# GNN sums with the features on the partitions: gathered rows as the stationary side, one addition per group of edges

## The chip, the cores and the metric

The kernel runs on one core of a Trainium2 chip. A core has five engines that run their own instruction streams and wait for each other by semaphores: PE (TensorE, matrix products; its weight loads are listed apart as PEld), DVE (VectorE), ACT (ScalarE), POOL (GpSimd) and SP (which here only issues transfers). A matrix product has a stationary side, which is loaded into PE, and a moving side, whose columns are streamed past it. The metric is the device time of one execution in microseconds (us).

## The reference

Two layers follow each other on 12500 nodes with 256 features each (`x`, f32). A sparse mixture of experts stands behind a graph convolution:

```
z   = layernorm(x)
agg = segment_sum(z[src] * edge_weight[:, None], dst, 12500)   # 200000 edges, dst sorted
x   = x + agg @ W.T + b
y   = layernorm(x)
# gate: graph attention over 131072 other edges gives each node scores for 4 experts,
# the two best of them get softmax weights
x   = x + sum over 4 experts of gate * (gelu(y @ W1 + b1) @ W2 + b2)   # 256 -> 512 -> 256
```

All of it is f32. The change concerns the second line and the product with `W` behind it. In the inputs the destinations are denser for small node numbers, so that a run of consecutive edges reaches few nodes.

## The kernel before

**Front** (0 to 141 us). The 200000 edges are cut into 1563 chunks of 128 and 261 groups of six chunks (`GQ`). `src`, `dst` and `edge_weight` are loaded and turned so that a chunk's edges lie on the 128 partitions. `x` is normalised in 25 groups of four tiles of 128 nodes (six buffers; loads on SP's queue, L93; statistics on DVE, L104) and written to the table `z_rows` in DRAM (L316). Woven into that loop stands `windows()` (L235), which works out on DVE, for each group of edges, the first node that it reaches, the tile of 128 nodes that this node lies in (`tile0`), each edge's place in a window of 128 places (`lo_q`: the node number modulo 128, raised by 128 where the edge lies 128 or more nodes beyond the first, so that it matches nothing), and two masks `in0` and `in1` that say which places of the window belong to that tile and which to the next one. It also counts groups that reach over more nodes than one window (`more`).

**Edge stage** (141 to 2223 us). For each group POOL issues six indirect gathers (`gt<-z_rows`, L550 in `prepare`), each of 128 rows of 256 f32; three groups' rows fit into the buffers. DVE builds the one-hot rows of the edges' places (`hit_w`, L340), ACT scales each by its edge's weight (`oh_w`, L556). In `product` (L564) PE adds up six products in one PSUM tile `win` of 128 places x 256 features, with the one-hot rows `oh_w` as the stationary side and the 256 features of the gathered rows moving. An f32 product runs as two instruction pairs of load and product. `add_window` (L571) then adds `win` to `acc_x`, the sums of all nodes (128 nodes of a tile on the partitions, 99 tiles, 256 features), twice per group: to tile a under the mask `in0`, and to tile a + 1 under `in1`. Between these steps the stage runs another work: a sort of the 131072 edges of the attention (`count_all`, then `sort_all`: L340, L428 to L498). The order on PE, DVE and ACT is written out by hand for this stage (`tc.manual_schedule`); POOL follows its own program order. Behind it stand a CAST of the sort's result (L608) and a branch (L614) for groups that reach beyond one window; no instruction of its body runs on these inputs.

**Node stage** (2231 to 2453 us). Its order is a scheduler's, from a loop over groups of four node tiles with lags:

```python
for g in range(NG + 3):
    for stage, lag in ((node_load, -2), (node_out, 1), (node_norm, 2), (node_turn_back, 3),
                       (node_turn, 0), (node_gat, 3)):
```

`node_load` loads `x` for two groups and adds the bias on POOL (L707). `node_turn` turns `acc_x` on PE (L686) and copies it out of PSUM on ACT (L687), into `agt`. `node_out` multiplies by the turned `W` (L725) and adds `x` on DVE (L727), then takes statistics (L104, L105). `node_norm` forms `y` on DVE (L739). `node_turn_back` turns `y` (L686, L687) and stores it. `node_gat` forms the attention's values (PE L753, DVE L756 to L762), stores them (L765), and issues four scatters per group on POOL (L767) into the table of segment starts.

**The rest** (2453 us to the end): a scan over the segment starts, the experts (PE is busy nearly throughout; POOL gathers the attention's rows, L809), and the weighted sum with its transfers.

Of the kernel before, what the change touches and what calls it, by code (L numbers as in the profile page):

```python
# [34 lines left out]
P = 128  # L35
# [25 lines left out]
def gnn_gat_moe(ctx, tc, x, src, dst, edge_weight, W, b, W_gat, att_src, att_dst, b_gat, ln_gamma,  # L61
# [98 lines left out]
    wide = tc.alloc_tile_pool(name="wide", bufs=1)  # L160
    acc_x = wide.tile([P, NT + 1, D], F32, name="acc_x")
    for k in range(0, NT + 1, 3):
        nc.gpsimd.memset(acc_x[:, k:k + 3, :], 0.0)
    with ExitStack() as s1:
# [61 lines left out]
        lo_q = edges.tile([P, NQ * GQ], BF, name="lo_q")  # L226
        tile0 = edges.tile([P, NQ + 1], I32, name="tile0")
        in0 = edges.tile([P, NQ], F32, name="in0")
        in1 = edges.tile([P, NQ], F32, name="in1")
        more = edges.tile([1, 5 * P], I32, name="more")  # L230
# [4 lines left out]
        def windows():  # L235


# [7 lines left out]
            nc.vector.tensor_copy(further_by, ahead)  # L245
            as_int = late.tile([P, NQ * GQ], I32, name="scratch")
            nc.vector.tensor_copy(as_int, dst_f)
            nc.vector.tensor_scalar(as_int, as_int, P - 1, None, ALU.bitwise_and)
            nc.vector.tensor_copy(lo_q, as_int)
            beyond = late.tile([P, NQ * GQ], F32, name="scratch")  # L250
            nc.vector.tensor_scalar(beyond, ahead.rearrange("p q j -> p (q j)"), float(P), float(P),
                                    ALU.is_ge, ALU.mult)
            nc.vector.tensor_add(lo_q, lo_q, beyond)
            nc.vector.tensor_copy(tile0[:, :NQ], first_f)
            within = late.tile([P, NQ], F32, name="within")
            as_int = late.tile([P, NQ * GQ], I32, name="scratch")
            nc.vector.tensor_scalar(as_int[:, :NQ], tile0[:, :NQ], P - 1, None, ALU.bitwise_and)
            nc.vector.tensor_copy(within, as_int[:, :NQ])
            nc.vector.tensor_scalar(tile0[:, :NQ], tile0[:, :NQ], 7, None, ALU.logical_shift_right)
            nc.vector.tensor_scalar(in0, within, part, None, ALU.is_le)  # L260
            nc.vector.tensor_scalar(in1, within, part, None, ALU.is_gt)

# [60 lines left out]
        for i in range(2):  # L323
            pt = bank()
            for o in range(2):
# [3 lines left out]
        nc.sync.dma_start(STARTS[:E2, :].rearrange("(p l) c -> p (l c)", p=P),  # L329
                          acc_x.rearrange("p t d -> p (t d)")[:, :L2 * SEG])  # L330

# [228 lines left out]
        def product(rows, hots, there):  # L560

            win = ps.tile([P, D], F32, name="win")
            for j, (r, h) in enumerate(zip(rows, hots)):
                i = nc.tensor.matmul(win, h, r, start=(j == 0), stop=(j == len(rows) - 1))  # L564
                if j == 0:
                    after_all(i, there)
            return win

        def add_window(at, win, m):
            to = acc_x[:, bass.ds(at, 1), :].rearrange("p o d -> p (o d)")  # L570
            return nc.vector.scalar_tensor_tensor(to, win, m, to, ALU.mult, ALU.add)  # L571

# [5 lines left out]
        with tc.manual_schedule(engines={mybir.EngineType.PE, mybir.EngineType.DVE,  # L578
                                         mybir.EngineType.Activation}):
            at, done, coming, win = (), 0, group(0), None  # L580
            for q in range(NQ + 1):
                was, win = win, product(*coming) if q < NQ else None
                if q:
                    a = at[(q - 1) % 4]
                    i0 = add_window(a, was, in0[:, q - 1:q])
                if q + 1 < NQ:
                    coming = group(q + 1)
                if q:
                    i1 = add_window(a + 1, was, in1[:, q - 1:q])
                    if q + 1 < NQ:  # L590
                        tc.declare_no_dep(i1.ins, i0.ins, reason="the next tile of nodes")
                if q < NQ and q % 4 == 0:
                    n = min(4, NQ - q)
                    _, at = nc.values_load_multi_w_load_instructions(
                        tile0[0:1, q:q + n], engines=(mybir.EngineType.DVE,), min_val=0,
                        max_val=NT - 1, skip_runtime_bounds_check_because=BOUND)
                for work, q0, q1, steps in parts:
                    if q == q0:
                        done = 0
                    while q0 <= q < q1 and done * (q1 - q0) < (q + 1 - q0) * steps:  # L600
                        next(work, None)
                        done += 1
            for work, *_ in parts:
                for _ in work:
                    pass
# [8 lines left out]
        with tc.If(further > 0):  # L614
            shift = edges.tile([P, 1], F32, name="shift")
            idx4 = edges.tile([P, GQ], I32, name="idx4")
            lo4 = edges.tile([P, GQ], F32, name="lo4")
            lob4 = edges.tile([P, GQ], BF, name="lob4")
            node4 = edges.tile([P, GQ], I32, name="node4")
            w4 = edges.tile([P, GQ], F32, name="w4")  # L620
            ahead4 = edges.tile([P, GQ], F32, name="ahead4")
            below4 = edges.tile([P, GQ], F32, name="below4")
            m01 = edges.tile([P, 2], F32, name="m01")
            with tc.For_i(0, NQ, 1) as q:
                nc.vector.memset(shift, 0.0)
                n = nc.values_load(more[0:1, bass.ds(q, 1)], min_val=0, max_val=NT,
                                   skip_runtime_bounds_check_because=BOUND)
                with tc.For_i(0, n, 1) as j:
                    nc.vector.tensor_scalar_add(shift, shift, float(P))
                    nc.vector.tensor_copy(idx4, src1[:, bass.ds(q * GQ, GQ)])  # L630
                    nc.vector.tensor_copy(w4, w1[:, bass.ds(q * GQ, GQ)])
                    nc.vector.tensor_copy(ahead4, further_by.rearrange("p q j -> p (q j)")[
                        :, bass.ds(q * GQ, GQ)])
                    nc.vector.tensor_copy(m01[:, 0:1], first_f[:, bass.ds(q, 1)])
                    nc.vector.tensor_scalar(lo4, ahead4, m01[:, 0:1], None, ALU.add)
                    nc.vector.tensor_copy(node4, lo4)
                    nc.vector.tensor_scalar(node4, node4, P - 1, None, ALU.bitwise_and)
                    nc.vector.tensor_copy(lo4, node4)
# [4 lines left out]
                    nc.vector.tensor_copy(m01[:, 0:1], in0[:, bass.ds(q, 1)])  # L643
                    nc.vector.tensor_copy(m01[:, 1:2], in1[:, bass.ds(q, 1)])
                    nc.vector.tensor_copy(lob4, lo4)
                    win = product(*prepare(idx4, lob4, w4, range(GQ)))
                    a = nc.values_load(tile0[0:1, bass.ds(q, 1)], engines=(mybir.EngineType.DVE,),
                                       min_val=0, max_val=NT - 1,
                                       skip_runtime_bounds_check_because=BOUND)
                    a = nc.s_assert_within(a + j + 1, 0, NT - 1, skip_runtime_bounds_check_because=BOUND)  # L650
                    add_window(a, win, m01[:, 0:1])
                    add_window(a + 1, win, m01[:, 1:2])

# [3 lines left out]
    with ExitStack() as s2:  # L657
# [51 lines left out]

        def node_turn(g):  # L710
            f, (t0, n, _) = flow[g], rows_of(g)
            f["agt"] = gp.tile([P, GT, 2, P], F32, name="agt", bufs=2)
            turn(lambda i: acc_x[:, t0 + i, :], n, f["agt"])

        def node_out(g):
# [5 lines left out]
            for i, m in pairs(n):  # L721
                po = ps.tile([P, 2, D], F32, name="po")
                for a in range(m):
                    for k in range(2):
                        nc.tensor.matmul(po[:, a, :], f["agt"][:, i + a, k, :], w_t[:, k, :],  # L725
                                         start=(k == 0), stop=(k == 1))
# [47 lines left out]
        node_load(1)  # L774
        for g in range(NG + 3):
            for stage, lag in ((node_load, -2), (node_out, 1), (node_norm, 2), (node_turn_back, 3),
                               (node_turn, 0), (node_gat, 3)):
                if 0 <= g - lag < NG and (lag >= 0 or g - lag >= 2):
# [425 lines left out]
```

## Time and profile before

| | |
|---|---|
| runs, us | 4192.93, 4193.42, 4193.94 (median 4193.42) |
| profiled execution, us | 4198.22 |
| its span, us | 4196.4 |
| its mean granted PE clock | 0.935 |
| busy over the span | PE 3552.0 us (85%), PEld 2610.1 (62%), DVE 2393.0 (57%), ACT 1421.4 (34%), POOL 2906.0 (69%) |

The lines that follow are from a page of one profiled execution and from queries of its trace. The page shows the span in 40 equal slices, with a digit for the busy tenths of each engine. A group line names the source line, the engine, the operation, output<-inputs and the count, then busy time and the mean duration of one in ns, then the idle time of the engine ahead of these instructions with what released it ("issue": nothing that the profile shows). A wait line gives the total, the number of waits and the longest, in us. A timeline line gives the start, the duration, engine, line, operation and shapes, and how many like instructions it joins ("x12"), with the idle time before it in brackets. All inner durations belong to this one execution.

### The profile page before, as it was taken

The numbers are of one execution on the slowest core, as the hardware profiler recorded it, in microseconds if no ns is written. First come the engines' busy times: TensorE is split into PE (matmuls) and PEld (weight loads), VectorE is DVE, ScalarE is ACT, GpSimd is POOL, SyncE is SP. The second block draws the span as 40 slices with busy tenths as digits, with TensorE's granted clock in tenths as the row PEclk, the third lists the DMA queues.
The fourth block names the chain that finished last, engine by engine and source line by source line (L and its number), as shares of the span: only waits on it lengthen the run. The fifth ranks groups of instructions, "written<-read, shape, count | busy, mean of one in ns | idle before, by whom it ended". The sixth has DMA issues, their size and how long they took to land. (4 is left out here: it accounts for less than half of the span.)

```text
span 4196.4 us, 54596 instructions
## 1 busy us (share of the span) xinstructions
PE 3552.0 (85%) x18969; PEld 2610.1 (62%) x18970; DVE 2393.0 (57%) x5474; ACT 1421.4 (34%) x3289; POOL 2906.0 (69%) x2855
## 2 busy tenths in 40 slices
PE   1466899999999999999998959999989999899545
PEld 0365676767766667767677836666656666566424
DVE  7566777878787878787778950221211202212477
ACT  4322445445545444545452211221212212212122
POOL 2577777777777777777776777777777777773440
PEclk6688999999999999999999969999999999999767
DMA  7433333333333333333335652222222222221698
GB/s 234 135 93 93 102 102 100 100 100 101 100 101 100 99 101 101 100 101 100 99 102 157 191 145 60 67 72 55 64 50 75 75 55 64 65 60 62 206 226 346
DMA packets 265845, 457.42 MB, mean 109 GB/s; under 512 B 67943, under 2 KB 168705, under 8 KB 264289
## 3 DMA queue, kind: packets, MB, share of 16 engines
q0 software_dynamic: 114128, 219.11, 21.4%
q1 hardware_dynamic: 111663, 207.52, 14.0%
q10 hardware_dynamic: 39778, 27.28, 2.1%
q8 instruction: 153, 2.51, 0.2%
q14 instruction: 123, 1.01, 0.1%
HBM read 334.05 MB, written 119.66 MB: 108 GB/s over the span
## 5 line engine op out<-in xcount | busy, mean ns | idle before, releaser
L550 POOL DMA_INDIRECT gt<-z_rows,src x1563 | 1605.2, 1027 | 592.2 <-issue 410.2
L809 POOL DMA_INDIRECT G<-gat_nodes,order x1024 | 1026.5, 1002 | 339.3 <-issue 289.0
L564 PE MATMUL win<-gt,oh_w 128*128 128x256 f32 x3126 | 770.1, 398 | 200.4 <-DMA gt<-z_rows,src 149.3
L564 PEld LDWEIGHTS win<-gt,oh_w 128*128 128x128 f32 x3126 | 598.0, 198 | 317.0 <-issue 188.4
L966 PE MATMUL po<-w,hh 128*128 128x256 f32 x3136 | 724.3, 385 | 51.4 <-ACT hh L948 38.3
L966 PEld LDWEIGHTS po<-w,hh 128*128 128x128 f32 x3136 | 605.5, 193 | 220.8 <-issue 87.1
L970 DVE TENSOR_TENSOR fo<-po,b 128x512 f32<-128x512 f32 x196 | 135.3, 690 | 1016.6 <-PE po L966 1016.6
L942 PE MATMUL ph<-yt,w 128*128 128x512 f32 (+1 forms) x1600 | 707.8, 586 | 2.8 <-DMA w<-in_L_ffn_W 2.8
L556 ACT ACTIVATE oh_w<-hit_w,w 128x128 f32<-128x128 bf16 x1563 | 500.9, 390 | 448.2 <-PE win L564 226.6
L490 DVE TENSOR_SCALAR st<-along,place_l,code 128x1024 bf16<-128x1024 f16 x1024 | 550.3, 578 | 162.3 <-PE perm L498 161.7
L948 ACT ACTIVATE hh<-ph,b 128x512 f32<-128x512 f32 (+1 forms) x400 | 249.3, 676 | 1001.6 <-PE ph L942 1001.5
L498 PE MATMUL perm<-st,to_p 128*128 128x512 bf16 x2048 | 524.1, 378 | 0.0
L942 PEld LDWEIGHTS ph<-yt,w 128*128 128x128 f32 x1600 | 305.0, 191 | 292.5 <-issue 277.9
L454 PE MATMUL look<-next,oht 98*128 98x128 f32 x2044 | 393.8, 300 | 0.0
L454 PEld LDWEIGHTS look<-next,oht 98*128 98x128 f32 x2044 | 309.6, 192 | 37.5
L462 ACT ACTIVATE next<-place 98x256 f32<-98x256 f32 x511 | 196.1, 384 | 345.1 <-PE place L459 344.3
L469 DVE TENSOR_TENSOR sel<-look,oh_lo 128x512 f32<-128x512 f32 x256 | 174.9, 683 | 186.4 <-PE look L454 185.2
L498 PEld LDWEIGHTS <-to_p 128*128 128x128 bf16 x2048 | 178.5, 97 | 122.3 <-DVE st L490 0.4
L571 DVE SCALAR_TENSOR_TENSOR acc_x<-win,in,acc_x 128x256 f32 x522 | 246.9, 473 | 8.7 <-PE win L564 8.6
L450 PE MATMUL look<-oh_lo,same_hi 128*128 128x128 bf16 x1024 | 228.1, 223 | 1.2 <-ACT next L462 1.0
L442 ACT ACTIVATE same_hi<-bank 128x512 bf16<-128x512 f32 x256 | 152.8, 597 | 215.2 <-PE bank L440 215.1
L340 DVE TENSOR_TENSOR oh_hi<-twice,hi 128x784 bf16<-128x784 bf16 x256 | 143.4, 560 | 100.6 <-PE place L364 100.5
(278 smaller groups left out, 3641.8 us busy)
## 6 DMA issues: line engine op xcount, KB each, us to landing
expert_rows<-fo SPq DMA_DIRECT2D x48, 1024.0 KB, 4.2
fo_in<-expert_rows SPq DMA_DIRECT2D x24, 2048.0 KB, 16.4
gt<-z_rows,src POOLq DMA_INDIRECT x1563
G<-gat_nodes,order POOLq DMA_INDIRECT x1024
xt<-in_x SPq DMA_DIRECT2D x24, 512.0 KB, 4.8
z_rows<-xt ACTq DMA_DIRECT2D x24, 512.0 KB, 4.6
x_two<-in_x SPq DMA_DIRECT2D x12, 1024.0 KB, 6.4
x_rows<-x_two SPq DMA_DIRECT2D x12, 1024.0 KB, 10.6
```

What stands on the lines that cost most here:

```text
L450: first = nc.tensor.matmul(look[:, i % GT + k, :], b["m"][:, i + k, :], one(b["ol"], i + k), start=True, stop=False)
L454: nc.tensor.matmul(look[:, i % GT + k, :], b["oht"][:, i + k, :], nxt[:, k, :], start=False, stop=True)
L490: last = nc.vector.tensor_scalar(st[:, k, :], along, b["l"][:, i + k:i + k + 1], code2[:, c:c + 1], ALU.is_equal, ALU.mult)
L498: first = nc.tensor.matmul(perm[:, h, :], one(b["p"], i + k), st[:, k, h * 512:(h + 1) * 512], start=(c == 0), stop=(c == NC2 - 1), skip_g ...
L550: there = [nc.gpsimd.indirect_dma_start(out=rows[j], out_offset=None, in_=Z, in_offset=IND(ap=idx[:, c:c + 1], axis=0)) for j, c in enumer ...
L556: there += [nc.scalar.activation(hots[j], one(hit, j), AF.Copy, scale=w[:, c:c + 1]) for j, c in enumerate(chunks)]
L564: i = nc.tensor.matmul(win, h, r, start=(j == 0), stop=(j == len(rows) - 1))
L571: return nc.vector.scalar_tensor_tensor(to, win, m, to, ALU.mult, ALU.add)
L809: i = nc.gpsimd.indirect_dma_start(out=G[:, t + 1, :], out_offset=None, in_=NODE, in_offset=IND(ap=order[:, t:t + 1], axis=0))
L942: i = nc.tensor.matmul(ph[:, :n], w_1[:, e, k, f * P:(f + 1) * P], yts[g][:, :n, k, :], start=(k == 0), stop=(k == 1))
L948: i = nc.scalar.activation(item["hh"][:, f, :n * P], ph[:, :n].rearrange("p t m -> p (t m)"), AF.Gelu, bias=b_1[:, e * NF + f:e * NF + f + 1])
L966: m = nc.tensor.matmul(po[:, a, :], item["hh"][:, f, i * P:(i + 1) * P], w_2[:, e, f, :], start=(f == 0), stop=(f == NF - 1))
```

## The change

`acc_x` is kept the other way round: 128 features on the partitions, two halves of features, and all nodes along the free dimension. In `product` the gathered rows are now the stationary side, one half of 128 features at a time, and the 128 scaled one-hot columns move. Each chunk so has two products of 128 columns where it had one of 256. A group's window starts exactly at its first node (`start`), at any place of the free dimension, so that `add_window` is one plain addition, without masks. `windows()` has less to work out: an edge's place is its distance from the first node. `node_turn` is gone, and the products of `node_out` read `acc_x` directly as their stationary side; the lags behind it are one smaller. The branch for far groups is shortened accordingly.

```diff
-    acc_x = wide.tile([P, NT + 1, D], F32, name="acc_x")
+    acc_x = wide.tile([P, 2, NPAD + P], F32, name="acc_x")
...
-            as_int = late.tile([P, NQ * GQ], I32, name="scratch")
-            nc.vector.tensor_copy(as_int, dst_f)
-            nc.vector.tensor_scalar(as_int, as_int, P - 1, None, ALU.bitwise_and)
-            nc.vector.tensor_copy(lo_q, as_int)
-            beyond = late.tile([P, NQ * GQ], F32, name="scratch")
-            nc.vector.tensor_scalar(beyond, ahead.rearrange("p q j -> p (q j)"), float(P), float(P),
-                                    ALU.is_ge, ALU.mult)
-            nc.vector.tensor_add(lo_q, lo_q, beyond)
-            nc.vector.tensor_copy(tile0[:, :NQ], first_f)
-            within = late.tile([P, NQ], F32, name="within")
-            as_int = late.tile([P, NQ * GQ], I32, name="scratch")
-            nc.vector.tensor_scalar(as_int[:, :NQ], tile0[:, :NQ], P - 1, None, ALU.bitwise_and)
-            nc.vector.tensor_copy(within, as_int[:, :NQ])
-            nc.vector.tensor_scalar(tile0[:, :NQ], tile0[:, :NQ], 7, None, ALU.logical_shift_right)
-            nc.vector.tensor_scalar(in0, within, part, None, ALU.is_le)
-            nc.vector.tensor_scalar(in1, within, part, None, ALU.is_gt)
+            nc.vector.tensor_copy(lo_q, ahead.rearrange("p q j -> p (q j)"))
+            nc.vector.tensor_copy(start[:, :NQ], first_f)
...
         def product(rows, hots, there):
-            win = ps.tile([P, D], F32, name="win")
+            win = ps.tile([P, 2, P], F32, name="win")
             for j, (r, h) in enumerate(zip(rows, hots)):
-                i = nc.tensor.matmul(win, h, r, start=(j == 0), stop=(j == len(rows) - 1))
-                if j == 0:
-                    after_all(i, there)
+                for k in range(2):
+                    i = nc.tensor.matmul(win[:, k, :], r[:, k * P:(k + 1) * P], h,
+                                         start=(j == k == 0), stop=(j == len(rows) - 1),
+                                         skip_group_check=True)
+                    if j == k == 0:
+                        after_all(i, there)
             return win
 
-        def add_window(at, win, m):
-            to = acc_x[:, bass.ds(at, 1), :].rearrange("p o d -> p (o d)")
-            return nc.vector.scalar_tensor_tensor(to, win, m, to, ALU.mult, ALU.add)
+        def add_window(at, win):
+            to = acc_x[:, :, bass.ds(at, P)]
+            return nc.vector.tensor_add(to, to, win)
...
                 if q:
-                    a = at[(q - 1) % 4]
-                    i0 = add_window(a, was, in0[:, q - 1:q])
+                    add_window(at[(q - 1) % 4], was)
                 if q + 1 < NQ:
                     coming = group(q + 1)
-                if q:
-                    i1 = add_window(a + 1, was, in1[:, q - 1:q])
-                    if q + 1 < NQ:
-                        tc.declare_no_dep(i1.ins, i0.ins, reason="the next tile of nodes")
...
-        def node_turn(g):
-            f, (t0, n, _) = flow[g], rows_of(g)
-            f["agt"] = gp.tile([P, GT, 2, P], F32, name="agt", bufs=2)
-            turn(lambda i: acc_x[:, t0 + i, :], n, f["agt"])
-
         def node_out(g):
...
-                        nc.tensor.matmul(po[:, a, :], f["agt"][:, i + a, k, :], w_t[:, k, :],
+                        nc.tensor.matmul(po[:, a, :],
+                                         acc_x[:, k, (t0 + i + a) * P:(t0 + i + a + 1) * P],
+                                         w_t[:, k, :],
                                          start=(k == 0), stop=(k == 1))
...
-        for g in range(NG + 3):
-            for stage, lag in ((node_load, -2), (node_out, 1), (node_norm, 2), (node_turn_back, 3),
-                               (node_turn, 0), (node_gat, 3)):
+        for g in range(NG + 2):
+            for stage, lag in ((node_load, -2), (node_out, 0), (node_norm, 1), (node_turn_back, 2),
+                               (node_gat, 2)):
```

The order that results in the changed kernel differs around the node stage. On DVE the CAST of the sort's result and the instruction behind it come after the branch, where the CAST stood ahead of it. On PE the products of three node groups (24 L725 products of f32) stand at the head of the stage. On POOL two bias additions (L707) with eight scatters (L767) behind them become one addition, one scatter, one addition, seven scatters.

More of the change, by code (lines that the diff above doesn't have):

```diff
@@ L160, in gnn_gat_moe @@
     wide = tc.alloc_tile_pool(name="wide", bufs=1)
-    acc_x = wide.tile([P, NT + 1, D], F32, name="acc_x")
+    acc_x = wide.tile([P, 2, NPAD + P], F32, name="acc_x")
+    acc_flat = acc_x.rearrange("p h n -> p (h n)")
     for k in range(0, NT + 1, 3):
-        nc.gpsimd.memset(acc_x[:, k:k + 3, :], 0.0)
+        nc.gpsimd.memset(acc_flat[:, k * D:(k + 3) * D], 0.0)
     with ExitStack() as s1:
@@ L226, in gnn_gat_moe @@
         lo_q = edges.tile([P, NQ * GQ], BF, name="lo_q")
-        tile0 = edges.tile([P, NQ + 1], I32, name="tile0")
-        in0 = edges.tile([P, NQ], F32, name="in0")
-        in1 = edges.tile([P, NQ], F32, name="in1")
+        start = edges.tile([P, NQ + 1], I32, name="start")
         more = edges.tile([1, 5 * P], I32, name="more")
@@ L329, in gnn_gat_moe @@
         nc.sync.dma_start(STARTS[:E2, :].rearrange("(p l) c -> p (l c)", p=P),
-                          acc_x.rearrange("p t d -> p (t d)")[:, :L2 * SEG])
+                          acc_flat[:, :L2 * SEG])
         s0.close()
@@ L594, in gnn_gat_moe @@
                     _, at = nc.values_load_multi_w_load_instructions(
-                        tile0[0:1, q:q + n], engines=(mybir.EngineType.DVE,), min_val=0,
-                        max_val=NT - 1, skip_runtime_bounds_check_because=BOUND)
+                        start[0:1, q:q + n], engines=(mybir.EngineType.DVE,), min_val=0,
+                        max_val=N - 1, skip_runtime_bounds_check_because=BOUND)
                 for work, q0, q1, steps in parts:
@@ L616, in gnn_gat_moe @@
             idx4 = edges.tile([P, GQ], I32, name="idx4")
-            lo4 = edges.tile([P, GQ], F32, name="lo4")
             lob4 = edges.tile([P, GQ], BF, name="lob4")
-            node4 = edges.tile([P, GQ], I32, name="node4")
             w4 = edges.tile([P, GQ], F32, name="w4")
@@ L622, in gnn_gat_moe @@
             below4 = edges.tile([P, GQ], F32, name="below4")
-            m01 = edges.tile([P, 2], F32, name="m01")
             with tc.For_i(0, NQ, 1) as q:
@@ L633, in gnn_gat_moe @@
                         :, bass.ds(q * GQ, GQ)])
[L634 to L638, printed above, removed]
                     nc.vector.tensor_scalar(ahead4, ahead4, shift, None, ALU.subtract)
@@ L642, in gnn_gat_moe @@
                     nc.vector.tensor_mul(w4, w4, below4)
-                    nc.vector.tensor_copy(m01[:, 0:1], in0[:, bass.ds(q, 1)])
-                    nc.vector.tensor_copy(m01[:, 1:2], in1[:, bass.ds(q, 1)])
-                    nc.vector.tensor_copy(lob4, lo4)
+                    nc.vector.tensor_copy(lob4, ahead4)
                     win = product(*prepare(idx4, lob4, w4, range(GQ)))
-                    a = nc.values_load(tile0[0:1, bass.ds(q, 1)], engines=(mybir.EngineType.DVE,),
-                                       min_val=0, max_val=NT - 1,
+                    a = nc.values_load(start[0:1, bass.ds(q, 1)], engines=(mybir.EngineType.DVE,),
+                                       min_val=0, max_val=N - 1,
                                        skip_runtime_bounds_check_because=BOUND)
-                    a = nc.s_assert_within(a + j + 1, 0, NT - 1, skip_runtime_bounds_check_because=BOUND)
-                    add_window(a, win, m01[:, 0:1])
-                    add_window(a + 1, win, m01[:, 1:2])
+                    a = nc.s_assert_within(a + j * P + P, 0, N - 1,
+                                           skip_runtime_bounds_check_because=BOUND)
+                    add_window(a, win)
     with ExitStack() as s2:
```

## The prediction

> **What bounds the kernel now.** I read the slices of the page first, then the groups and waits of the long middle stretch, then timelines of one group of edges and of one pair of node groups, and last the front.
>
> ```profile
> PE   1466899999999999999998959999989999899545
> POOL 2577777777777777777776777777777777773440
> ```
>
> A slice is 105 us. PE looks like the bound from slice 5 on, but POOL's 7 is also flat over slices 2 to 20, the edge stage (141 to 2223 us). The groups of POOL in the window 400 to 2200 us and the waits of POOL and PE there decide between them:
>
> ```profile
> L550 POOL DMA_INDIRECT gt<-z_rows,src x1364 | 1385.0, 1015 | 415.7 <-issue 357.8 <-DMA gt<-z_rows,src 19.8 <-PE place L459 13.1
> ```
> ```profile
> POOL gt L550 <- issue: 410.2, 1346, 0.3
> ```
> ```profile
> PE win L564 <- DMA gt<-z_rows,src: 111.9, 102, 2.3
> PE win L564 <- issue: 28.1, 34, 1.7
> ```
>
> Busy 1385.0 plus gaps 415.7 make 1800.7 us of a window of 1800, and no gap is longer than 0.3: POOL issues gather after gather, 1.320 us each, 7.92 us for a group of six. It never waits for a buffer, an index or PE. PE waits for the rows: 111.9 + 28.1 = 140 us over some 227 groups, 0.6 us each. So the edge stage is paced by the issue of 1563 gathers, which the change leaves alone; PE has a slack of 0.5 to 0.6 us a group, DVE more (busy 1421 of 1800). One group on PE and DVE, from the timeline:
>
> ```profile
> 2171.09 0.47 DVE L571 SCALAR_TENSOR_TENSOR acc_x<-win,in,acc_x 128x256 f32 x1
> ...
> 2173.64 2.46 PEld L564 LDWEIGHTS win<-gt,oh_w 128*128 128x128 f32 x12 [1.14 <-issue]
> ...
> 2173.67 2.83 PE L564 MATMUL win<-gt,oh_w 128*128 128x256 f32 x12 [0.99 <-DMA gt<-z_rows,src]
> ```
>
> Twelve load-and-product pairs of 256 columns take 2.83 us, 0.236 each. The node stage (2231 to 2453) is another matter: between 2253 and 2440 DVE is busy 182.3 of 187 us.
>
> **The change part by part.** *The products.* Six chunks with two halves, each f32 product still two pairs, give 24 pairs of a 128-wide load and 128 moving columns, where there were 12 with 256. Nearest rows, from timelines:
>
> ```profile
> 2170.42 0.22 PE L450 MATMUL look<-oh_lo,same_hi 128*128 128x128 bf16 x1
> 2170.48 0.44 PE L454 MATMUL look<-next,oht 98*128 98x128 f32 x2
> 2170.75 0.23 PE L450 MATMUL look<-oh_lo,same_hi 128*128 128x128 bf16 x1
> ```
> ```profile
> 2231.50 1.94 PE L686 MATMUL pt<-ident,acc_x 128*128 128x128 f32 x16 [1.47 <-DVEq L614]
> ...
> 2339.13 1.86 PE L753 MATMUL ph<-wg,yt 128*128 128x16 f32 x16
> ```
>
> L450 and two L454, three pairs of 128 columns, repeat after 0.33 us: 0.11 each. The sixteen turns of L686, each with a new f32 load and 128 columns, take 1.94, 0.121 each; L753, with 16 columns, is limited by loads, 0.116 each. So 24 pairs cost 2.78 to 2.90 us: −0.05 to +0.07 a group against 2.83, inside PE's 0.5. Worth nothing. Upper bound: if the load does not hide at all, a pair costs the whole 0.22 of L450's or half L454's row plus nothing else; that is 24 x 0.22 = 5.28, a rival below.
>
> *The additions.* 261 of 522 L571 go, 261 x 0.473 = 123 us of DVE, all beside POOL's gathers; what hides it is that gather stream, and uncovered it would be worth those 123 us. The remaining addition reads the same 128x256; its form (plain addition, two rows of 128 nodes) is new, and the nearest row, L727 with 0.69 for 512 columns, does not make it dearer than 0.47. A gather's busy time does depend a little on DVE (0.95 while DVE is idle, 1.015 in the mean), but the gathers beside L571 look like those without; I take 0, with ±10 for the whole stage from shifted coincidences. The last window's second addition and one CAST (below) do lie on the path.
>
> *The window table.* Removed from DVE: L247 0.976, L248 0.967, L249 0.966, L251 0.942, L253 1.778, L257 to L261 0.286 + 0.287 + 0.268 + 0.348 + 0.349 = 7.17 us; added: one CAST of 128x1566 f32 to bf16, 0.97 by L249's row. Net −6.2, in a stretch (40 to 70 us) where DVE has no idle time. Later DVE waits for x:
>
> ```profile
> DVE st L104 <- DMA xt<-in_x: 15.1, 10, 3.3
> ```
>
> Loads of x follow the release of six buffers, which follows the LN arithmetic, so some of the shift is passed on and some is lost in these waits. I take −4, bounds 0 and −6.2.
>
> *The boundary.* The order of the changed kernel puts the CAST of the permutation behind the branch, beside the node stage's first loads, and the last group has one addition.
>
> ```profile
> 2230.07 1.23 DVE L608 CAST st<-perm 128x1024 bf16<-128x1024 f32 x1 [0.22 <-PE perm L498]
> ...
> 2239.89 9.29 POOL L707 TENSOR_TENSOR x_two<-x_two,b_all 128x1024 f32<-128x1024 f32 x4 [17.22 <-DMA b_all<-in_L_gnn_b]
> ...
> 2242.27 0.69 DVE L727 TENSOR_TENSOR x_two<-x_two,po 128x512 f32<-128x512 f32 x1 [9.94 <-POOL x_two L707]
> ```
>
> The branch waits for it, and the issue of b_all's load follows; so up to 1.23 + 0.47 = 1.7 is gained, and I take 1.5, least 0. The first turns and copies are gone as well, but they were hidden: the first L727 waits for POOL's addition of b_all, not for PE.
>
> *The node stage.* Gone are the L686 turns of acc_x (196 instructions, 25.3 us of PE) and their 49 copies (26.7 us of ACT). Neither engine sets the pace. L725 reads acc_x directly, with the same loads. Two groups cost 16.96 us between like rows of DVE:
>
> ```profile
> 2329.77 0.69 DVE L727 TENSOR_TENSOR x_two<-x_two,po 128x512 f32<-128x512 f32 x1
> ...
> 2339.94 5.27 DVE L739 TENSOR_SCALAR y<-x_two,mv,rstd 128x256 f32<-128x256 f32 x1
> 2346.73 0.69 DVE L727 TENSOR_TENSOR x_two<-x_two,po 128x512 f32<-128x512 f32 x1
> ```
> ```profile
> 2340.40 4.65 POOL L707 TENSOR_TENSOR x_two<-x_two,b_all 128x1024 f32<-128x1024 f32 x2
> 2346.41 0.99 POOL L767 DMA_INDIRECT gat_starts<-nds,seg  x1 [1.36 <-DVE root L119]
> ```
>
> One normalisation, 0.38 elsewhere, takes 5.27: it stands until both of POOL's additions are over. So DVE's full time hides 4.9 us of standing still per two groups, while POOL in turn waits 1.36 + 1.28 for DVE before its scatters (8 x 1.27 = 10.2 us, and 4.65). With the lags one shorter, POOL's order becomes addition, one scatter, addition, seven scatters: DVE can work during the first scatter, and a second instruction can be caught. I take 0.6 us a pair of groups (half of that scatter's 1.27), 12 pairs: −7. Best case: POOL alone paces, 10.2 + 4.65 = 14.8, −2.1 x 12 = −25. Worst, both additions now catch DVE after it has had to wait for an addition: +0.7 x 12 = +8. The scatters' end releases the starts' load, the scans and the experts (PE again from 2494.9), with nothing else late, so the shift reaches the end. The run of experts and the mix are unchanged.
>
> Sum: −4 + 0 − 1.5 − 7 = −12.5, on the profiled execution's 4198.2 (span 4196.4): 4185.7. It lies 4.8 above the median of the runs, 4193.4, which goes to **4181**.
>
> **The rivals.** *Loads that do not hide (slower).* With the gathered rows stationary, every load is 128 columns for a product of only 128. PE's slack decides: (2.83 + 0.5) / 24 = 0.139 us a pair. At 0.16, 24 x 0.16 = 3.84, 0.5 beyond the slack, x 229 groups of the sorting part = +115; at 0.22, 1.95 x 229 = +445, about 4640. For: L564's product of 256 columns covers its next load twice over, one of 128 just once, with nothing to spare. Against: the rows above, all at or below 0.121. The Trainium skill, "TensorE: Matmul & The Clock Gate", Part 3 "Packing small matmuls — row/col tiling", The mechanism, says that a weight load overlaps running products only where their row groups differ, which full-height pairs never do; by it load and product would run one after the other, 4640. The trace disagrees: a pair with 16 columns takes 0.116 (L753), one with 128 takes 0.121 (L686), so the 112 further columns lie beside a load. I give 0.06 to a real slowdown here.
>
> *A node stage with a new pace (slower).* The PE rows are not always at full rate: L725 takes 3.70 us a group at 2340 but 5.39 at 2332 and 9.10 for two groups at 2237. Without 25.3 us of turns PE rests more. If L725 stays at 5.39 and PE, ahead of the turn back and the scatters, takes DVE's place: +1.7 x 25 = +42, 4223. Together with POOL's additions coming too late for L727 (the +8 above): 0.14.
>
> *No measurable difference.* The front is lost in waits for x and the additions hold DVE as long as before: −1 to −4, or the gathers' coincidences (+5) offset the node stage. 0.25; 4190.
>
> *The change doesn't do what it says.* If windows now spanned over 128 nodes more often, the extra branch would run; but its condition comes from the same distances as before, and no instruction of it stands in the trace. Nothing for this.
>
> **How the numbers follow.** A measurement of this kernel can tell about 0.2%, 8.4 us. My forecast, faster by 8.5 to 30 us, has 0.54; no measurable difference 0.25 (within 8.4 on either side); slower 0.21: loads 0.06, node stage 0.14, gathers beyond +8.4 0.01. The range: all gains at their best, −6.2 − 1.7 − 25 = −33, less likely together than alone, so −30: 4163. Upwards +8 of the node stage or +10 of the gathers with nothing gained is about +10: 4203. That leaves out the large rivals and the extremes, about 2 in 10. The likeliest case's own range is 4163 to 4185.
>
> **What would show it.** Right: in the changed profile, gathers still back to back at 1.32 us and PE waiting for rows some 0.5 us a group; the 24 pairs in 2.7 to 2.9 us; first gather near 137 instead of 141.18; two node groups in 16.3 instead of 16.96 with the longest normalisation below 5 us. Wrong: gaps in POOL's gathers released by PE; pairs above 0.139 us; gathers with another mean than 1.02 (0.01 us each is 16 us of the total); node groups longer than 17 us per two, with DVE waiting for PE's L725 or for POOL.

## The result and the profile after

The changed kernel takes 4134.86 us in the median of four runs (4133.34 to 4137.45), against 4193.68 for the kernel before in the same comparison: a ratio of 0.986, 95% interval 0.9845 to 0.9874. That is 59 us less, where 12.5 were forecast, and below the range. The profiled execution has a span of 4134.4 us; 62.0 us are gone from the span. In the changed kernel the gathers stand at L534, the products at L550, the addition at L559, the one-hot rows at L324, and in the node stage L680, L693, L709, L723 and L737 answer to L707, L725, L739, L753 and L767.

The slices of PE and POOL on the changed kernel's page are nearly those of before. From the first gather to the end of the last one (each from the trace), the edge stage lasts 2032.8 us instead of 2081.5. The stretches add up to the 62 us so: start of the first gather 141.2 before and 135.6 after (−5.6); gathers −48.7; last gather to last scatter 229.8 and 226.8 (−3.0); from there to the end 1744.0 and 1739.3 (−4.7). The group of the gathers from 400 to 2100 us shows the stage:

```profile
L534 POOL DMA_INDIRECT gt<-z_rows,src x1325 | 1298.3, 980 | 403.5 <-issue 338.9 <-PE place L443 23.1 <-PE win L550 15.2
```

Busy and gaps fill the window again (1701.8 of 1700), and the waits of POOL still show no gap over 0.3 us behind the first gather: POOL paces the stage as before. What has changed is one gather: 980 ns instead of 1015 (1015 was the mean from 400 to 2200), over the whole kernel 996 instead of 1027. 1563 x 31 ns = 48 us.

```profile
POOL gt L534 <- issue: 394.7, 1296, 0.3
```

PE's side is as forecast. From the timeline of PE, and its waits from 400 to 2100:

```profile
1503.95 2.92 PE L550 MATMUL win<-oh_w,gt 128*128 128x128 f32 x24 [0.86 <-DMA gt<-z_rows,src]
```
```profile
PE win L550 <- DMA gt<-z_rows,src: 60.7, 74, 2.1
PE win L550 <- issue: 18.3, 29, 2.3
```

24 pairs take 2.84 (at 1512.55) to 2.92 us, 0.12 each; PE still waits for rows, 79 us over some 220 groups, 0.36 each where it was 0.6.

### The profile page after: what moved, and what is told of

The parts are those of the page before. It is cut to its first block, busy times and chain, and to the rows that moved or that the text cites. A ratio compares the mean times of both kernels' runs of the same rounds, so it can differ in the third digit from the quotient of the medians.

```text
span 4134.4 us, 59517 instructions
## 1 busy us (share of the span) xinstructions
PE 3557.3 (86%) x21899; PEld 2727.4 (66%) x21900; DVE 2231.6 (54%) x5204; ACT 1397.5 (34%) x3240; POOL 2855.5 (69%) x2855
## 5 line engine op out<-in xcount | busy, mean ns | idle before, releaser
L534 POOL DMA_INDIRECT gt<-z_rows,src x1563 | 1556.8, 996 | 586.3 <-issue 394.7
L550 PE MATMUL win<-oh_w,gt 128*128 128x128 f32 x6252 | 793.3, 286 | 131.1 <-DMA gt<-z_rows,src 99.2
L550 PEld LDWEIGHTS win<-oh_w,gt 128*128 128x128 f32 x6252 | 755.6, 200 | 166.4 <-issue 157.7
L474 DVE TENSOR_SCALAR st<-along,place_l,code 128x1024 bf16<-128x1024 f16 x1024 | 540.2, 569 | 192.5 <-PE perm L482 192.5
L324 DVE TENSOR_TENSOR oh_hi<-twice,hi 128x784 bf16<-128x784 bf16 x256 | 143.5, 560 | 115.7 <-PE place L348 115.6
L455 DVE TENSOR_REDUCE pos<-sel 128x4 f32<-128x512 f32 x256 | 175.6, 686 | 8.8
```

The lines of the kernel that those rows point to most:

```text
L474: last = nc.vector.tensor_scalar(st[:, k, :], along, b["l"][:, i + k:i + k + 1], code2[:, c:c + 1], ALU.is_equal, ALU.mult)
L534: there = [nc.gpsimd.indirect_dma_start(out=rows[j], out_offset=None, in_=Z, in_offset=IND(ap=idx[:, c:c + 1], axis=0)) for j, c in enumer ...
L550: i = nc.tensor.matmul(win[:, k, :], r[:, k * P:(k + 1) * P], h, start=(j == k == 0), stop=(j == len(rows) - 1), skip_group_check=True)
```

## The experiments

Wherever a gather's loss is told below, it is worked out from the trace: a gather that meets nothing takes 945 ns; what it takes beyond that is its loss, and it is put to the DVE operation that runs 60 ns after its start (of two that overlap, the later one). Before, 1563 gathers lose 128.2 us in all, after 79.8: the difference, 48.4, is nearly all of the edge stage's 48.7. By operation, before and after, in us: oh_lo 33.8 and 34.6; hit_w 24.5 and 6.7; st 25.0 and 20.1; to_p 20.9 and 5.6; oh_hi 19.1 and 10.9. Beside sel, pos and with DVE idle a gather loses 4 ns or less, beside the addition 17 ns before and 0 after. So nearly all of the loss stands beside one-hot rows and st, operations that the change does not touch.

**One operation more, another form, one operation less, other pairs.** Four kernels in one comparison. The first adds to the changed kernel

```diff
                 if q + 1 < NQ:
                     coming = group(q + 1)
+                if q:
+                    to = acc_x[:, :, bass.ds(at[(q - 1) % 4], P)]
+                    nc.vector.scalar_tensor_tensor(to, was, none, to, ALU.mult, ALU.add)
```

> The changed kernel with a second addition per group put back where the old kernel had it (behind hit_w): the same window again, times a column of zeros, 261 additions more on DVE. Theory A (the gathers were held up less because DVE has one operation less per group between the 16-bit operations): the gathers' mean goes from 996 ns back to 1015 to 1030, the time from 4135 to 4165 to 4185. Theory B (the masked form of the addition held the gathers up) gives part of that or all of it, since the operation put back has that form. Theory C (PE's 24 short pairs shifted the meeting of gathers and DVE): gathers stay at 996, the time within 8 of 4135.

(`none` is a column of zeros.) Measured: 4181.74 us, ratio to the kernel before 0.9962 (0.9948 to 0.9976), 47 us more than the changed kernel took; gathers 1024 ns, their loss 123.0 us. Differences to the changed kernel go across comparisons, here and below; the kernel before took 4193.7 to 4197.4 us in these, but for one comparison on another chip, named below.

The second keeps one addition and gives it the old form:

```diff
-            return nc.vector.tensor_add(to, to, win)
+            return nc.vector.scalar_tensor_tensor(to, win, ones[:, 0:1], to, ALU.mult, ALU.add)
```

> The changed kernel with its one addition in the old form (window times a column of ones, plus sums). Theory A: gathers at 990 to 1005 ns, time 4130 to 4145. Theory B: the gathers go half of the way back, 1010 ns or more, time 4155 or more. Theory C: as A.

Measured: 4133.63 us, ratio 0.9847 (0.9831 to 0.9864), gathers 995 ns. The form is nothing; theory B falls.

The third takes the second addition from the kernel before:

```diff
-                if q:
-                    i1 = add_window(a + 1, was, in1[:, q - 1:q])
-                    if q + 1 < NQ:
-                        tc.declare_no_dep(i1.ins, i0.ins, reason="the next tile of nodes")
```

> The kernel before without its second addition (the sums that fall into the next tile of nodes are left out). Theory A: the gathers' mean falls from 1027 to about 1000 ns, the time from 4193 to 4145 to 4160. Theory B: half of it, about 4170. Theory C: nothing, 4193 within 8.

Measured: 4157.59 us, ratio 0.9902 (0.9885 to 0.9918), gathers 1002 ns, their loss 89.1 us.

The fourth splits the products of the kernel before into halves:

```diff
-                i = nc.tensor.matmul(win, h, r, start=(j == 0), stop=(j == len(rows) - 1))
+                for k in range(2):
+                    i = nc.tensor.matmul(win[:, k * P:(k + 1) * P], h, r[:, k * P:(k + 1) * P],
+                                         start=(j == k == 0), stop=(j == len(rows) - 1),
...
```

> The kernel before with each product split into two halves of 128 columns, one-hot rows still stationary: 24 pairs per group. Theory A and B: no change of the gathers, 4193 within 8, the group of pairs 2.8 to 2.9 us long. Theory C: the gathers' mean falls to about 1000 ns, time about 4150.

Measured: 4201.8 us, ratio 1.0008 (0.9998 to 1.0017), gathers 1029 ns, the 24 pairs 2.92 us long. The 24 pairs cost and bring nothing; theory C falls. Most of the edge stage's gain is the second addition's, from both sides: put back, it makes the stage 43 us longer (2076.1), and without it the stage of the old kernel is 39 us shorter (2042.1). Where the remaining 5 to 9 of the 48.7 us come from is not shown. But the addition's own 123 us of DVE were hidden, and gathers lose little beside it. What moved are the losses beside other operations, so the next kernels ask what those are and when they hit.

**Order, count, data type.** The third edit below only exchanges two lines; the second has the same extra addition as above in another place.

```diff
-    twice = first_two.tile([P, P, 2], BF, name="twice")
+    twice = first_two.tile([P, P, 2], F32, name="twice")
```

> The changed kernel with the table that the four kinds of one-hot rows (hit_w, oh_hi, oh_lo, to_p) are compared with in f32 instead of bf16. The comparison of a mixed pair should run at the rate of the mixed addition L253 (1.135 ns per element of a row, against 0.68 in bf16), so DVE gets some 2 us more work per two groups. Theory A1 (a gather that begins while DVE is in an operation on 16-bit data alone is held until shortly before that operation's end): the 58 us that gathers lose beside the four kinds fall to under 10, the gathers' mean from 996 to 955 to 970 ns, the time to 4080 to 4100. Rival (what holds a gather is how busy DVE is, whatever the data): gathers at 1000 ns or more, time 4135 or more.

Measured: 4376.96 us, ratio 1.0428 (1.0411 to 1.0445), gathers 1149 ns; a gather that meets oh_lo (now 1217 ns long) loses 823 ns in the mean, where it lost 279.

Theory A1 falls: an operation need not work on 16-bit data alone to hold a gather. The rival falls as well: gathers beside sel and with DVE idle still lose 0 to 1 ns. A comparison with the table in f32 holds gathers too, and longer, as it runs longer. What the one-hot rows share in both types, and sel, pos and the addition lack, is that both tensors that they read lie in SBUF. (st lacks it as well and yet holds gathers; more of it below.)

```diff
                 if q:
                     add_window(at[(q - 1) % 4], was)
+                    to = acc_x[:, :, bass.ds(at[(q - 1) % 4], P)]
+                    nc.vector.scalar_tensor_tensor(to, was, none, to, ALU.mult, ALU.add)
```

> The second addition of zeros again, but right behind the first one, ahead of hit_w. If the number of operations decides (A2): as with it behind hit_w, gathers 1024 ns, time 4175 to 4190. If the place decides (A3): another loss, between 4135 and 4170 or above 4190.

Measured: 4159.29 us, ratio 0.9916 (0.9899 to 0.9932), gathers 1007 ns.

```diff
-                if q:
-                    add_window(at[(q - 1) % 4], was)
                 if q + 1 < NQ:
                     coming = group(q + 1)
+                if q:
+                    add_window(at[(q - 1) % 4], was)
```

> The changed kernel with the order of two DVE operations exchanged: hit_w of the next group ahead of the addition of the last window, not behind it. The number of operations stays. If the number of DVE operations per group decides (A2), nothing moves: 4135 within 8. If what decides is where DVE's 16-bit operations fall against the starts of gathers (A3), the gathers' mean moves by 6 ns or more in either direction, the time by 10 us or more.

Measured: 4164.59 us, ratio 0.9926 (0.991 to 0.9943), gathers 1009 ns. The same operations in another order cost 30 us, as much as a whole operation more in one place (24) and less than in the other (47). So A3: not the number of DVE's operations decides but where they fall against the starts of gathers.

**Two tensors from SBUF.** The addition itself can be made one of these:

```diff
+                    held = hot.tile([P, 2, P], F32, name="held")
+                    nc.scalar.activation(held, was, AF.Copy)
-                    add_window(at[(q - 1) % 4], was)
+                    add_window(at[(q - 1) % 4], held)
```

> The changed kernel, but ACT first copies each window from PSUM to SBUF, and the same addition on DVE reads both operands from SBUF. Theory A4 (a gather is held by a DVE operation that reads two tensors from SBUF, whatever their type; an addition that reads the window from PSUM holds nothing): gathers that begin beside the addition, 0 ns longer before, are now 100 ns or more longer in the mean, 10 us or more in sum, and the gathers' mean rises from 996 ns to 1003 or more. Rival (it is the broadcast comparison that holds them): the gathers beside the addition stay within 20 ns of 945.

This comparison ran on another chip, on which the kernel before takes 4975.64 us, so its times stand only against that one: 4876.97 us, ratio 0.9814 (0.9773 to 0.9854). POOL there often waits for PE (362 us for the products), and only 37 gathers meet the addition; they lose 112 ns each, 4.1 us in sum. The 100 ns are reached, the 10 us in sum and the gathers' mean of 1003 (it is 999) are not. Once more on a chip like the first:

> The addition that reads the window from a copy in SBUF, once more, since PE's waits were long in the first run of it and few gathers met the addition there. A4: gathers that begin beside the addition 80 ns or more above 945, against 0 with the window in PSUM; the gathers' mean 1000 ns or more and the time 4140 or more. Rival: within 20 ns of 945, 4135.

Measured: 4150.7 us, ratio 0.9899 (0.9882 to 0.9915), gathers 1012 ns. 83 gathers meet the addition and lose 122 ns each, 10.1 us, against 0 ns with the window in PSUM. The shape, type and operation are the same; what has changed for DVE is where one operand lies. One of these gathers, the first line of DVE, the second of POOL:

```profile
918.50 0.41 DVE L559 TENSOR_TENSOR acc_x<-acc_x,held 128x256 f32 x1
```
```profile
918.64 1.09 POOL L534 DMA_INDIRECT gt<-z_rows,src  x1 [0.30 <-issue]
```

A4 holds for the addition. The Trainium skill says it in "SBUF — State Buffer", Who interferes with whom: a DVE instruction with two SBUF inputs contends with a GpSimd instruction that reads SBUF, since its second input comes through an interface that the two share. These rows agree, 122 ns against 0. Of the 24 us by which the losses of all gathers rose (79.8 to 104.1), these 10 stand beside the addition; the others moved once more, beside to_p (5.6 to 13.2) and st (20.1 to 29.0) above all.

One row pair from the timeline of the kernel before shows the length of a hold. The first line is of DVE, the second of POOL:

```profile
1499.55 0.54 DVE L340 TENSOR_TENSOR hit_w<-twice,lo_q 128x768 bf16<-128x768 bf16 x1
```
```profile
1499.65 1.41 POOL L550 DMA_INDIRECT gt<-z_rows,src  x1 [0.30 <-issue]
```

hit_w ends at 1500.09; the gather, begun 0.10 after it, takes 1.41 instead of 0.95: 0.46 more, about what was left of hit_w. In the changed kernel the loss is mostly 0.12 to 0.13 us less than what is left: with 0.585 us of oh_lo left a gather loses 0.460, with 0.495 of to_p 0.371, with 0.373 of hit_w 0.249.

Two tensors from SBUF are not the only thing that holds a gather. st reads one, beside two columns of scalars, and it held this one in the changed kernel, with DVE idle for 0.96 us behind it:

```profile
2098.71 1.00 DVE L474 TENSOR_SCALAR st<-along,place_l,code 128x1024 bf16<-128x1024 f16 x2
```
```profile
2099.32 1.21 POOL L534 DMA_INDIRECT gt<-z_rows,src  x1 [0.31 <-issue]
```

0.39 us were left of the second st, and 0.26 were lost. Why st holds gathers, no run here tested; beside it stand 20.1 of the changed kernel's 79.8 us.

**Shorter operations.** If a gather waits for the end of what it meets, shorter operations should hold it less. First each row of a block alone, against a scalar:

```diff
-            nc.vector.tensor_tensor(
-                t, twice[:, None, :width, :].to_broadcast(shape),
...
+            for i in range(n):
+                nc.vector.tensor_scalar(t[:, i, :], freeb[:, :width], v[:, i:i + 1], None,
+                                        ALU.is_equal)
```

> The changed kernel with each block of one-hot rows built by six or eight short DVE operations (one row of 128 or 98 numbers against one scalar, one tensor from SBUF) instead of one comparison of two tensors. If a gather is held until shortly before the end of the one operation that it meets, short operations hold it for 0.1 us at most: the 58 us lost beside one-hots fall to 5 to 20, the gathers' mean to 960 to 975 ns, the time to 4085 to 4110, if DVE's total stays under PE's and POOL's pace. Rival (each operation holds a gather anew): gathers at 996 ns or more, 4135 or more.

On the same chip as add_from_sbuf: 5082.65 us, ratio 1.0224 (1.0173 to 1.0276). The loss beside one-hots is 16 us, as expected, the gathers' mean 977 ns, just above its range. But these operations also read one tensor from SBUF where the comparison read two, so the run cannot tell which of the two changes took the loss away. And a short operation takes 265 ns (oh_lo, 128x128), so DVE's total grew; POOL waits for PE longer than in the other two kernels that ran there (566 us for the products from 142 to 2300, against 362 and 264). Over the whole kernel:

```profile
L536 POOL DMA_INDIRECT gt<-z_rows,src x1563 | 1527.1, 977 | 1272.9 <-PE win L552 669.5
```

Then the comparison of two tensors, in pieces of two chunks and of four:

```diff
...
+            for k in range(0, n // 2, 1):
+                m = min(1, n // 2 - k)
+                nc.vector.tensor_tensor(
+                    t[:, k:k + m], twice[:, None, :width, :].to_broadcast([P, m, width, 2]),
+                    v[:, k:k + m], ALU.is_equal)
```

(In the version by four chunks the step and the 1 in `min` are 2.)

> The changed kernel with each block of one-hot rows built in pieces of two chunks (four pieces of the blocks of eight, three of hit_w), by the same comparison of two tensors. If a gather waits only for the end of the one operation that it meets (A5), it is held 0.15 us at most where it was 0.6: the 58 us lost beside one-hots fall to 12 to 25, the gathers' mean from 996 to 965 to 975 ns, the time from 4135 to 4085 to 4110; DVE gets about 1 us more work per two groups, which it has. If each operation holds a gather anew, or the whole run of them does (A6): no gain, 4130 or more.

Measured: 4256.92 us, ratio 1.0148 (1.0131 to 1.0165), gathers 1073 ns. The losses rise to 200.3 us, 166 of it beside oh_lo and oh_hi. From the timelines of DVE and POOL in the counting part of the sort, early in the stage:

```profile
249.82 0.89 DVE L327 TENSOR_TENSOR oh_lo<-twice,lo 128x256 bf16<-128x256 bf16 x4
...
252.81 0.89 DVE L327 TENSOR_TENSOR oh_lo<-twice,lo 128x256 bf16<-128x256 bf16 x4
253.62 0.41 DVE L561 TENSOR_TENSOR acc_x<-acc_x,win 128x256 f32 x1
```
```profile
250.35 4.17 POOL L536 DMA_INDIRECT gt<-z_rows,src  x1 [0.30 <-issue]
```

A gather that begins at 250.35 takes 4.17 us: it gets in only at 253.6, when the addition, with its window from PSUM, ends a run of pieces without a gap. So A5 holds for an operation that stands by itself, and A6 for these short ones back to back.

> The same with pieces of four chunks (two pieces each). A5: about half of the 58 us is left, gathers 975 to 990 ns, time 4100 to 4125. A6: 4130 or more.

Measured: 4109.7 us (4103.53 to 4111.19), ratio 0.9796 (0.978 to 0.9813), gathers 979 ns, loss 52.5 us instead of 79.8, of it 36 beside one-hots:

```profile
L536 POOL DMA_INDIRECT gt<-z_rows,src x1563 | 1529.5, 979 | 586.1 <-issue 399.1
```

This version is faster than both kernels, by 25 us than the changed one; here too some gathers are held through two pieces. Why a run of 0.28 us pieces can keep a gather out to its end, when a gather mostly gets in behind an oh_lo of 0.68 though oh_hi follows, is open.

**The front.** Five wide operations of the old window table are put back, their result overwritten:

```diff
+            nc.vector.tensor_copy(as_int, dst_f)
+            nc.vector.tensor_scalar(as_int, as_int, P - 1, None, ALU.bitwise_and)
+            nc.vector.tensor_copy(lo_q, as_int)
...
+            nc.vector.tensor_add(lo_q, lo_q, beyond)
             nc.vector.tensor_copy(lo_q, ahead.rearrange("p q j -> p (q j)"))
```

> The changed kernel with the five wide operations of the old window table put back (L247, L248, L249, L251, L253 of the kernel before, 5.63 us by its profile), their result overwritten. If DVE's time there passes to the first gather undiminished: first gather 5 to 6 us later, at 141 to 142 us, time 4140. If the loads of x hide it: first gather within 2 us of 136.

On the same chip as add_from_sbuf: 4891.0 us, ratio 0.9847 (0.9802 to 0.9891), first gather at 141.6 us; its neighbours there began at 135.7 and 128.1, so nothing sure follows. Again, on a chip like the first:

> The five wide operations of the window table put back, beside the others of this call: first gather 5 to 6 us after theirs if DVE's time there passes on undiminished, within 2 us if the loads of x hide it.

Measured: 4141.84 us, ratio 0.988 (0.9863 to 0.9896), first gather at 141.5, against 135.8 and 135.3 with the one-hot rows in pieces and 135.6 in the changed kernel: 5.7 to 6.2 us for 5.63 of DVE. The front passes on, as far as one execution of each tells: in the other kernels with the changed front that leave it alone the first gather begins between 135.3 and 137.7 on chips like the first, and with the additional buffer of add_from_sbuf_again at 129.4; why was not followed up.

**The node stage.** The turns of acc_x are put back on PE, without copies and without use:

```diff
+            for i, m in pairs(n):
+                pt = ps.tile([P, 2, 2, P], F32, name="pt", bufs=4)
...
+                        nc.tensor.transpose(
+                            pt[:, a, k, :],
+                            acc_x[:, k, (t0 + i + a) * P:(t0 + i + a + 1) * P], ident)
```

> The changed kernel with the turns of acc_x put back on PE in the node stage (196 of them, into PSUM, not copied, not used). In the changed kernel two groups take 15.4 us where L693 runs 14 pairs in 3.27 us, and 18.2 where it takes 6.07. Theory N1 (without the turns PE rests and is at a lower clock in each second pair of groups): two groups at 15.4 to 16 throughout, node stage 8 us shorter or more, time 4120 to 4130. Theory N2 (the rate has another cause): pairs of 18 remain, and the turns cost up to 10 us: 4135 to 4145.

Measured: 4148.98 us, ratio 0.9889 (0.9873 to 0.9906), 14 us more than the changed kernel; from the first addition of x on DVE to the last scatter it takes 220.3 instead of 208.5, two groups 16.4 to 19.5. N1 falls. The turns cost 12 us here, but the order of the stage moved with them (long normalisations are back, 38.5 us of standing still), so this is not the price of PE's work alone.

## Why the prediction was wrong

*The additions* is the step that failed: "the gathers beside L571 look like those without; I take 0, with ±10 for the whole stage from shifted coincidences". The first half was right (17 ns). The term was mis-sized: taking one operation out shifted all others, and the coincidences were worth 48 us of the edge stage, of which the runs put 39 to 43 to the second addition. The profile had the material: gathers of 1.41 us beside hit_w. The sum of the gathers' losses, 128 us, was the bound to take for this term, instead of 10. The prediction's own list of what would show it wrong had the place: gathers with another mean than 1.02 us, 16 us for each 0.01; it became 0.996.

Shown are the source (the second addition, for most of it), that gathers are held by DVE operations in progress (the one-hot rows, st, an addition with both tensors in SBUF), and that place decides. to_p shows how: before, 56 of the 64 gathers that met it began inside it, 0.19 us behind its start for the most part, and lost 372 ns each; after, 62 of 77 began within 0.03 us of its start and lost 1 ns. Which place results from an edit stays unforeseen: why the gathers begin there now, and why hit_w meets 42 after and 118 before, was not settled.

*POOL paces the stage, PE's 24 pairs fit*: right, 0.12 us a pair, 2.84 to 2.92 a group, no gap. The rival with loads that do not hide falls, as before_24_pairs shows too.

*The window table*: −4 forecast, −5.6 measured at the first gather, within the bounds of 0 and −6.2; the waits for x took little or nothing.

*The boundary*: −1.5 forecast; from the last gather to the first addition of x 19.6 us before and 18.3 after, −1.3. Variants of the changed kernel that leave this part alone show 18.1 to 20.4, so the agreement is not clear of their scatter.

*The node stage*: −7 forecast, 210.2 to 208.5 measured, −1.7, within bounds. Variants of the changed kernel that leave the stage alone show 198.6 to 209.8, the kernel before and its variants 210.2 to 213.0: a gain, but one execution of each does not tell its size. The mechanism was right in part: no normalisation is long any more (98 in 35.0 us instead of 88.6), but shorter operations now stand still in their place: L111 and L122 take 36.7 us instead of 8.3, single ones 2.95 where 0.16 is usual. One of these, from 2276.41 to 2279.36, ends with POOL's addition L680, which runs from 2276.98 to 2279.33.

Two groups take 15.4 us in some pairs and some 18 in others, where L693's fourteen instructions take 6.07 instead of 3.27 and POOL waits for DVE:

```profile
2268.22 3.27 PE L693 MATMUL po<-w_t,acc_x 128*128 128x256 f32 x14
...
2285.66 6.07 PE L693 MATMUL po<-w_t,acc_x 128*128 128x256 f32 x14
...
2287.35 0.96 POOL L737 DMA_INDIRECT gat_starts<-nds,seg  x1 [2.77 <-DVE nds L732]
```

The granted clock of PE was 1.00 from 2264 to 2280 us and 0.55 from 2280 to 2291.5. So the second rival, PE as the pace in a part of the pairs, was half there; what lowers the clock in these is open.

*After the last scatter* nothing was forecast and 4.7 us are missing. The kernel before and its two variants range there from 1737.2 to 1744.3, the changed one and its variants on chips like the first from 1738.1 to 1744.2; that it is due to the change is not shown.

## What to carry to other kernels

Where POOL issues indirect transfers back to back and paces a stage, sum up how much longer they take than the undisturbed one, by the DVE operation that runs at their start: that sum is what any edit of DVE's order may move, also one that is "hidden". In this kernel, operations that read two tensors from SBUF hold POOL's gathers until they, and at times their run, end; st, with one such tensor, does so too. An operand in PSUM took the addition's hold away, and pieces of 0.42 us a third of all losses. A price of nothing for a removed operation needs the question what shifts when it is gone.

## What was not expected of the hardware

A gather of 0.95 us was held to 4.17 us by comparisons of 0.25 to 0.29 us each that followed each other without a gap, while halves of 0.42 us instead of whole blocks of 0.68 cut the losses from 79.8 to 52.5 us. An addition that read its window from SBUF instead of PSUM held gathers by 122 ns instead of 0. A comparison with an f32 table, 1.22 us long instead of 0.68, held them by 823 ns instead of 279.
